# First layer's weight products moved into the adjacency build, and the last 96 nodes updated in three sets of 32

## The chip, the cores and the metric

The kernel runs on one core of a Trainium2 chip. The metric is the device time of one execution in microseconds (us). Before the change the median of 6 runs is 1797.62 us (1793.65 to 1804.84). In the profile the engines are PE (TensorE matmul), PEld (TensorE weight load), DVE (VectorE), ACT (ScalarE), POOL (GpSimd) and SP (SyncE).

## The reference, cut to what matters

A graph of 625 nodes with 512 features and 20000 edges, sorted by destination, goes through four layers, each on the normalised features of the one before, with a residual. All arrays are float32.

```python
edge_index = jnp.stack([src, dst])
h = jnp.maximum(_layernorm(x, axis=-1), 0.0)
x = x + _L0_gnn_ref(h, edge_index, L0_gnn_W, L0_gnn_b)
h = jnp.maximum(_layernorm(x, axis=-1), 0.0)
x = x + _L1_gnn_ref(h, src, dst, edge_type_8, edge_weight, ...)   # relational, two sublayers
h = jnp.maximum(_layernorm(x, axis=-1), 0.0)
x = x + _L2_gnn_ref(h, edge_attr_4, edge_attr_8, edge_index, ...)
h = jnp.maximum(_layernorm(x, axis=-1), 0.0)
x = x + _L3_gnn_ref(h, edge_index, edge_attr_64, ...)
```

Layer 0 (SAGE with the mean):

```python
    neighbor_mean = neighbor_sum / neighbor_count[:, None]
    h = jnp.concatenate([x, neighbor_mean], axis=-1)
    return h @ W.T + b
```

Layer 3 (messages of edges, then an update of nodes):

```python
    h = mish(edge_feat @ W1 + b1)
    messages = mish(h @ W2 + b2)
    agg = jax.ops.segment_sum(messages, dst, num_segments=x.shape[0])
    u = mish(jnp.concatenate([x, agg], axis=-1) @ W3 + b3)
    out = u @ W4 + b4
    y = x + out
    ...                         # layer norm of y with gamma and beta
```

## The kernel before

Nodes lie in 5 chunks (NC) of 125 (P), edges in 160 tiles (NT) of 125, features in 4 chunks (KD) of 128. The order of instructions on an engine is chosen by a scheduler at compile time, which goes by the written order and takes a later instruction where an earlier one isn't ready in its model. Instructions wrapped in `keep(...)` hold their written order on their engine. The matmuls are not wrapped; nearly everything of VectorE and ScalarE in the parts below is.

**The build of the adjacency** (`layers01_near`, lines 436 to 581). Sixteen stages of ten edge tiles make eight weighted adjacency matrices (`adj`) and one plain count of edges (`cnt`), source by destination. For each tile VectorE makes a one-hot of the sources (`ohs`, line 556, six buffers) and for five tiles at a time a right side `rh` (line 547, three buffers); PE adds 15 products of them (line 538) into five PSUM banks, one for each chunk of sources. PSUM has eight banks in this part, all in one pool with the tag `q`. When a stage is done, ScalarE copies the new columns of its banks into `adj` and `cnt` (`copied`, line 507) and VectorE adds the columns that overlap with the stage before (`added`, line 519). In written order that happens in the next stage: after its second one-hot the copies and the additions for chunks 0 and 1, after its fourth the additions for chunks 2 to 4. PE does the first three tiles of a stage for chunks 0 to 2 first, then for chunks 3 and 4. In stages 0, 1, 4, 7 and 10 the copying is preceded by a zero fill of a block of columns on ScalarE (`zeroed`, line 497). Stage 0 also makes the edges' coefficients (`coefficients`, line 457). At its end x is loaded (line 234) and the small weights of layer 2 (`layer2_weights`, 16 loads on SP). At the ends of stages 8 and 9 x is normalised: statistics on VectorE (line 242), square root and relu on ScalarE (lines 244 and 252).

**Layer 0** (lines 583 to 619). After the build the weights W are loaded, h is transposed (line 264, copied by line 265), the neighbours are counted by 25 products of `cnt` with a column of ones (line 595), the neighbours' sums are made transposed, 40 products of h with `cnt` (line 606, in 512 and 113 columns), and 40 products with the two halves of W (line 613) follow; VectorE scales by the reciprocal count and adds to x.

**Layer 1** (lines 621 to 673) normalises x, transposes it, loads its weights (`loop` and four of `basis`, 1 MB each) when the pools of layer 0 are released, and begins with the products of line 637.

**Layer 3** (`layer3_near`) runs over 40 groups of four edge tiles, software-pipelined over steps s: `first(s)` makes z (lines 1327 and 1332), `second(s-2)` its product with W2 (line 1346), `sent(s-4)` sums messages by destination for a window of 32 nodes (line 1370, four matmuls side by side in columns of the array), `collected(s-5)` transposes them into `mT` (lines 1380 and 1381). mish is made as z times a quotient: a bounded copy (`bounded`, line 1291) goes through Exp, Ln(1+.) and Tanh on ScalarE (`quotients`, lines 1299 to 1303), and VectorE multiplies (lines 1468 and 1477). The last group is done in two halves (lines 1490 to 1493, multiplied by line 1361). The node update of a chunk follows when its last window is in: `update_u` (line 1391, the mish of it by `quotients` and `update_mul`), `update_turn` (transpose), `update_out` (line 1422, with the layer norm's statistics) and `update_root`/`update_end` (norm and output). Chunks 0 to 3 are updated between steps; the last chunk of 125 nodes when all groups are done.

Of the kernel before, what the change touches and what calls it, by code (L numbers as in the profile page):

```python
# [194 lines left out]
def gnn_body(ctx: ExitStack, tc: tile.TileContext, a: dict, out: bass.AP, consts, near: bool):  # L195
# [34 lines left out]
    hT = node.tile([128, KD, N], F32, tag="hT", name="hT")  # L230
# [16 lines left out]
    def norm_relu(h, c, stats, keep=lambda i: i):  # L247
        mv, rstd = stats
        off = work.tile([P, 1], F32, tag="off1", name="off1", bufs=NC)
        keep(nc.vector.reciprocal(rstd, rstd))  # L250
        keep(nc.vector.scalar_tensor_tensor(off, mv[:, 0:1], -1.0, rstd, op0=ALU.mult, op1=ALU.mult))
        nc.scalar.activation(h[:, c, :], x[:, c, :], AF.Relu, bias=off, scale=rstd)
# [177 lines left out]
    def layers01_near(wts2):  # L430
# [5 lines left out]
        with tc.tile_pool(name="adjacency", bufs=1) as bp:  # L436
            adj = bp.tile([P, NC, NQ, N], F32, name="adj")
            with tc.tile_pool(name="counts", bufs=1) as cp:
                cnt = cp.tile([P, NC, N], F32, name="cnt")
                with tc.tile_pool(name="build", bufs=2) as lp, \  # L440
# [16 lines left out]
                    def coefficients(k0):  # L457
                        ks = slice(k0, min(k0 + 4, K))
                        n = ks.stop - k0
                        oh_r = lp.tile([128, 4, P], F32, tag="oh_r", name="oh_r")  # L460
# [16 lines left out]
                    eq = lp.tile([P, NT, WT], BF16, name="eq", bufs=1)  # L477

# [28 lines left out]
                    def copied(s):  # L507


                        if s in zeros:  # L510
                            zeroed(s)
# [7 lines left out]
                    def added(s, cs):  # L519
# [4 lines left out]
                        for c in cs:  # L524
                            for dst, v in ((adj[:, c, :, at][:, :, lo:hi], done[s][c][:P, :NQ, lo:hi]),
                                           (cnt[:, c, at][:, lo:hi], done[s][c][:P, NQ, lo:hi])):
                                keep(nc.vector.tensor_add(dst, v, dst))

                    for s in range(NS):
# [14 lines left out]
                        for j0, j1 in zip(parts_of, parts_of[1:]):  # L544
# [6 lines left out]
                            if s == 0 and j1 < GS:  # L551
                                hots(j1, 2 * j1 if j1 < 8 else NT)
                                coefficients(j1)
                            for j in range(j0, j1):
# [13 lines left out]
                                if s > 0 and j == 3:  # L568
                                    added(s - 1, (2, 3, 4))
                        if s == NS - 1:  # L570
                            copied(s)
                            added(s, range(NC))
                        if s == 0:
                            load_rest()
                            w2s = layer2_weights(wts2)
                        if s == NS // 2:
                            h = node.tile([P, NC, D], F32, tag="h", name="h")
                            stats = [norm_stats(c, keep) for c in range(NC)]
                        if s == NS // 2 + 1:
                            for c in range(NC):  # L580
                                norm_relu(h, c, stats[c], keep)

                with tc.tile_pool(name="layer0n", bufs=2) as lp, banks("z", 8):
                    w0 = [lp.tile([128, KD, D], F32, name=f"w0{i}", bufs=1) for i in range(2)]
                    for i in range(2):
                        nc.sync.dma_start(w0[i], chunks(a["L0_gnn_W"][i * D:(i + 1) * D, :]))
                    b0 = lp.tile([P, D], F32, name="b0", bufs=1)
                    nc.sync.dma_start(b0, bcast(a["L0_gnn_b"], D))
                    for c in range(NC):
                        transposed(hT, h[:, c, :], c)  # L590
                        nc.vector.tensor_add(x[:, c, :], x[:, c, :], b0)
                    pc = ps("pc")
                    for c in range(NC):
                        for s in range(NC):
                            nc.tensor.matmul(pc[:P, c:c + 1], cnt[:, s, c * P:(c + 1) * P], ones,
                                             start=s == 0, stop=s == NC - 1)
                    rc = lp.tile([P, NC], F32, tag="rc", name="rc")
                    nc.vector.tensor_scalar_max(rc, pc[:P, :NC], 1.0)
                    nc.vector.reciprocal(rc, rc)

                    sT = lp.tile([128, KD, N], F32, name="sT", bufs=1)
                    for f in range(KD):
                        for n0, n1 in ((0, 512), (512, N)):
                            p = ps("nsum")
                            for s in range(NC):
                                nc.tensor.matmul(p[:, :n1 - n0], h[:, s, f * 128:(f + 1) * 128],
                                                 cnt[:, s, n0:n1], start=s == 0, stop=s == NC - 1)
                            nc.scalar.copy(sT[:, f, n0:n1], p[:, :n1 - n0])
                    for c in range(NC):
                        for i, v in enumerate((hT, sT)):  # L610
                            p = ps("l0")
                            for k in range(KD):
                                nc.tensor.matmul(p[:P, :], v[:, k, c * P:(c + 1) * P], w0[i][:, k, :],  # L613
                                                 start=k == 0, stop=k == KD - 1)
                            if i == 0:
                                nc.vector.tensor_add(x[:, c, :], p[:P, :], x[:, c, :])
                            else:
                                nc.vector.scalar_tensor_tensor(x[:, c, :], p[:P, :], rc[:, c:c + 1], x[:, c, :],
                                                               op0=ALU.mult, op1=ALU.add)

            with tc.tile_pool(name="layer1n", bufs=1) as lp, banks("y", 3):
# [989 lines left out]
```

## Time and profile before

| | |
|---|---|
| median of 6 runs | 1797.62 us |
| the profiled execution's own time | 1803.98 us |
| its span (first to last instruction) | 1802.1 us |
| mean granted TensorE clock | 0.972 |
| PE / DVE / ACT / POOL busy | 1703.7 / 1012.3 / 761.6 / 809.8 us |
| last product of the build, first product of layer 1 on PE | 170.53, 251.29 us |
| last record of line 1346 (second products of layer 3) ends | 1763.6 us |

In the answers below a row of a timeline has the start and the length in us, the engine, the line of the kernel, the operation, what it writes and reads, the shape and how many instructions were merged; in brackets the idle time of the engine before it and what ended it. A row of the chain of waits has start, length, engine, tile and line. A row of a table by stretches has the stretch, its length, and for PE, PEld, DVE, ACT and POOL the busy time and the number of instructions, then the granted clock (1.00 is full), the DMA engines' busy share and GB/s. In a row of groups the last part is the idle time before its instructions. A float32 matmul of the program is two records in the profile.

### The profile page before, as it was taken

How to read it: one execution, taken by the hardware profiler on the slowest of the kernel's cores; microseconds unless marked ns; L12 is line 12 of the kernel's file. 1: busy time of each engine (PE TensorE's matmuls, PEld its weight loads, DVE VectorE, ACT ScalarE, POOL GpSimd, SP SyncE). 2: the span in 40 equal slices, each digit the busy share in tenths (PEclk: the TensorE clock that was granted, in tenths of full speed). 3: DMA queues.
4: the chain of work that ended last, by engine and by line, in shares of the span. 5: the costliest groups of instructions: out<-in, count | busy, mean ns of one | idle time of the engine just before them, and what ended most of it. 6: DMA issues, size and time to landing. Idle time of an engine off the chain costs nothing.

```text
span 1802.1 us, 24375 instructions
## 1 busy us (share of the span) xinstructions
PE 1703.7 (95%) x9770; PEld 882.1 (49%) x9770; DVE 1012.3 (56%) x1697; ACT 761.6 (42%) x792; POOL 809.8 (45%) x479
## 2 busy tenths in 40 slices
PE   4888999999999889999999899999999999999995
PEld 4878544444444334444554445445444544444443
DVE  7997110001000378877953666876676676667663
ACT  2352010000000312222213677776676777767664
POOL 0000000000000277665715788888887788778300
PEclk9999899999999789999999899999999999999997
DMA  2001030020000186757535588666675676667300
GB/s 74 3 3 54 1 122 24 0 93 6 0 0 0 53 203 169 174 148 168 144 90 143 102 159 154 124 129 111 114 137 111 115 133 120 109 112 140 51 1 14
DMA packets 157220, 162.59 MB, mean 90 GB/s; under 512 B 97547, under 2 KB 104060, under 8 KB 157097
## 3 DMA queue, kind: packets, MB, share of 16 engines
q0 software_dynamic: 131584, 119.48, 33.9%
q1 hardware_dynamic: 20100, 32.69, 5.9%
q10 hardware_dynamic: 5412, 8.77, 1.7%
q8 instruction: 79, 1.29, 0.3%
q14 instruction: 45, 0.36, 0.1%
HBM read 155.11 MB, written 5.12 MB: 89 GB/s over the span
## 4 chain that ended last, share of the span: by engine, by line
PE 85%; DVE 5%; DMA 3%; issue 3%; ACT 2%; POOL 1%; DVEq 0%; ACTq 0%; POOLq 0%; SPq 0%
PE z L1346 27%; PE agg L661 10%; PE hb L648 8%; PE sum L961 6%; PE tpw L938 4%; PE q L538 4%; PE z L1332 4%; PE z L1327 4%; PE mlp L890 2%; PE xsd L1040 2%; PE agg L637 2%; PE agg L1370 2%; PE l L613 2%; DMA g_s<-xd,dst_i 2%; POOL g_s L281 1%
## 5 line engine op out<-in xcount | busy, mean ns | idle before, releaser
L1346 PE MATMUL z<-wm,z 128*125 128x512 f32 x1280 | 558.2, 594 | 2.7 <-DVE z L1465 2.7
L1346 PEld LDWEIGHTS z<-wm,z 128*125 128x125 f32 x1280 | 238.1, 189 | 294.1 <-issue 270.8
L281 POOL DMA_INDIRECT g_s<-xs,src_i x160 | 300.2, 1876 | 124.1 <-issue 75.6
L281 POOL DMA_INDIRECT g_s<-xd,dst_i x144 | 304.4, 2114 | 46.0 <-issue 42.0
L902 POOL MEMSET mT<- 128x5000 f32 x1 | 4.3, 4265 | 589.9 <-PE tr L843 589.9
L281 POOL DMA_INDIRECT gup<-up,src_i x160 | 196.6, 1229 | 109.7 <-issue 39.7
L1348 DVE TENSOR_TENSOR mess<-z,b 125x512 f32<-125x512 f32 x160 | 106.3, 686 | 137.3 <-PE z L1346 137.3
L661 PE MATMUL agg<-hb,adj 125*125 125x512 f32 x400 | 173.6, 592 | 0.0
L651 DVE COPY hb<-hb 125x512 f32<-125x512 f32 x20 | 13.8, 691 | 263.0 <-PE hb L648 263.0
L945 DVE TENSOR_TENSOR msg<-tpw,gup 125x768 f32<-125x768 f32 x160 | 151.3, 945 | 0.0
L1334 DVE TENSOR_SCALAR z<-z,b 128x500 f32<-128x500 f32 (+1 forms) x164 | 108.4, 719 | 73.4 <-PE z L1332 71.6
L538 PE MATMUL q<-rh,ohs 125*128 125x96 bf16 (+1 forms) x2400 | 120.4, 213 | 27.6 <-DVE ohs L556 26.4
L1299 ACT ACTIVATE uz<-uz 128x2000 f32<-128x2000 f32 (+1 forms) x41 | 75.0, 1830 | 154.2 <-DVE uz L1291 154.2
L648 PE MATMUL hb<-basis,hT 128*125 128x512 f32 x320 | 138.6, 592 | 0.0
L538 PEld LDWEIGHTS <-ohs 125*128 125x128 bf16 x2400 | 115.4, 101 | 32.7 <-DVE ohs L556 32.4
L961 PE MATMUL sum<-msg,ohy 125*32 125x256 f32 (+2 forms) x1600 | 124.5, 389 | 0.0
L653 ACT COPY hb<-hb 125x512 f32<-125x512 f32 x20 | 11.7, 585 | 260.2 <-PE hb L648 240.2
L661 PEld LDWEIGHTS agg<-hb,adj 125*125 125x125 f32 x400 | 74.8, 188 | 94.7 <-issue 94.7
L961 PEld LDWEIGHTS sum<-msg,ohy 125*32 125x32 f32 x1600 | 74.2, 109 | 84.3 <-issue 58.7
L1299 ACT ACTIVATE um<-um 125x2048 f32<-125x2048 f32 x39 | 74.5, 1910 | 71.1 <-DVE um L1291 71.1
L938 PE MATMUL tpw<-w,hid 64*125 64x512 f32 x320 | 97.3, 649 | 5.6 <-DVE msg L945 5.6
L943 DVE TENSOR_TENSOR msg<-tpw,gup 125x256 f32<-125x256 f32 x160 | 66.4, 415 | 63.6 <-PE tpw L938 55.5
(210 smaller groups left out, 2221.2 us busy)
## 6 DMA issues: line engine op xcount, KB each, us to landing
rt<-in_edge_attr SPq DMA_DIRECT2D x76, 125.0 KB
basis<-in_L_gnn_basis SPq DMA_DIRECT2D x8, 1024.0 KB
gup<-up,src_i POOLq DMA_INDIRECT x160, 5.6
g_s<-xs,src_i POOLq DMA_INDIRECT x160, 7.9
g_s<-xd,dst_i POOLq DMA_INDIRECT x144, 8.9
w<-in_L_gnn_W SPq DMA_DIRECT2D x2, 1024.0 KB
loop<-in_L_gnn_loop SPq DMA_DIRECT2D x2, 1024.0 KB
w1ab<-in_L_gnn_W ACTq DMA_DIRECT2D x1, 2048.0 KB
```

The costliest lines, as they stand in the source:

```text
L281: return nc.gpsimd.indirect_dma_start(out=dst, out_offset=None, in_=table, in_offset=bass.IndirectOffsetOnAxis(ap=idx[:, t:t + 1], axis=0) ...
L538: nc.tensor.matmul(q[c][:, :n, o:o + WT], hot[j][:, c, :], rhs[j][:, q0:q0 + n, :], start=j + k == 0, stop=j == GS - 1 and k == 2, skip_gr ...
L648: nc.tensor.matmul(p[:P, :], hT[:, k, s * P:(s + 1) * P], basis[b][:, k, :], start=k == 0, stop=k == KD - 1)
L661: nc.tensor.matmul(acc[c], adj[:, s - 1, l * NB + b, c * P:(c + 1) * P], hb[:, b, :], start=False, stop=s == NC and b == NB - 1)
L938: nc.tensor.matmul(p[:P, :], hid[s // 2][s % 2][rws, i * P:(i + 1) * P], w4[rws].rearrange("p k u -> p (k u)"), start=True, stop=True)
L945: nc.vector.tensor_mul(m[:, :, 1:, :], pv[:, 2:4, None, :].to_broadcast([P, 2, 3, MUL]), g[:, None, 1:, :].to_broadcast([P, 2, 3, MUL]))
L961: nc.tensor.matmul(A[r * W:(r + 1) * W, cs, :], oh[:, j, q, :], v, start=j % G == 0 and r not in done, stop=j % G == G - 1, skip_group_che ...
L1299: keep(nc.scalar.activation(u, u, AF.Exp))
L1327: nc.tensor.matmul(pf[f][:, :ne], w[half, f * 128:(f + 1) * 128], rt[half, cols], start=True, stop=False)
L1334: keep(nc.vector.tensor_scalar(zv[:, n, f, :], pf[f][:, :ne], b1[:, f:f + 1], None, op0=ALU.add))
L1346: nc.tensor.matmul(p[:P, :], z[:, j // w, f, j % w * P:(j % w + 1) * P], wm2[:, f, :], start=f == 0, stop=f == KD - 1)
L1348: keep(nc.vector.tensor_add(m[:, j, :], p[:P, :], bc["b2"]))
```

## The change

*In layers 0 and 1.* x is loaded a second time, as h, at the start, and both halves of W as well; ScalarE makes h's statistics (sums through `accum_out`), and the relu of h runs in stage 0. In stage 1 h is transposed. The products h·Wb and h·Wa, ten units of four matmuls, are put behind tiles 4, 6, 8 and 9 of stages 2 to 10, the tenth unit behind the build; ScalarE copies each unit out of PSUM, h·Wb over h and h·Wa into `own`. After the build the plain counts are multiplied with h·Wb, and a column of ones beside it gives the number of neighbours. Layer 1's weights are asked for before that, and its products read another layout of the transposed features (`hTc`). The storage of `cnt` is reused for layer 1's `hb`; that of W's second half for the small weights of layer 2, which are loaded at the end of stage 8.

*In layer 3.* The last chunk is split: its first 29 nodes are updated as a chunk of their own between the steps, and the other 96 in three sets of 32, each set's product with W3 as soon as its window is in, with the four blocks of features side by side in the array. The rest of their update (mish, transpose, output) is made at once at the end. The last group's mish is done in three pieces instead of two; for the group before it a table set is loaded ahead and the bounded copy stands ahead of the multiplication of the group before that.

```diff
+                h1 = node.tile([P, NC, D + 1], F32, tag="h", name="h")
+                h = h1[:, :, :D]
...
+                nc.sync.dma_start(h, a["x"].rearrange("(c p) d -> p c d", p=P))
...
+                nc.sync.dma_start(w0b, chunks(a["L0_gnn_W"][D:, :]))
...
+                    nc.sync.dma_start(w0a, chunks(a["L0_gnn_W"][:D, :]))
...
                     def copied(s):
-                        if s in zeros:
+                        if s > 0 and s in zeros:
                             zeroed(s)
...
+                    zeroed(0)
...
+                    keep(nc.gpsimd.memset(h1[:, :, D:], 1.0))
+                    for c in range(NC):
+                        keep(nc.scalar.activation(h[:, c, :], h[:, c, :], AF.Copy, accum_out=sums[:, c:c + 1]))
+                    keep(nc.scalar.mul(sums, sums, -1.0 / D))
...
+                        keep(nc.scalar.activation(junk[:P], h[:, c, :], AF.Square, bias=sums[:, c:c + 1],
+                                                  accum_out=var[:, c:c + 1]))
+                    keep(nc.scalar.activation(var, var, AF.Sqrt, bias=eps, scale=1.0 / D))
+                    def normed():
+                        keep(nc.vector.reciprocal(var, var))
+                        keep(nc.vector.tensor_mul(sums, sums, var))
+                        for c in range(NC):
+                            keep(nc.scalar.activation(h[:, c, :], h[:, c, :], AF.Relu, bias=sums[:, c:c + 1],
+                                                      scale=var[:, c:c + 1]))
+                    def turned(c):
+                        p = pp.tile([128, 512], F32, tag="q", name="tr")
+                        for k in range(KD):
+                            nc.tensor.transpose(p[:, k * P:(k + 1) * P], h[:, c, k * 128:(k + 1) * 128],
+                                                ident[:P, :P])
+                        keep(nc.scalar.copy(hTc[:, c, :, :P],
+                                            p[:, :KD * P].rearrange("p (k n) -> p k n", k=KD)))
+                    products = [(i, c) for i in range(2) for c in range(NC)]
+                    def product(k, at_end=False):
+                        i, c = products[0]
+                        if k == 0:
+                            unit["p"] = pp.tile([128, 512], F32, tag="q", name="hw")
+                        p = unit["p"]
+                        nc.tensor.matmul(p[:P, :], hTc[:, c, k, :P], (w0a if i else w0b)[:, k, :],
+                                         start=k == 0, stop=k == KD - 1)
+                        if k == KD - 1:
+                            keep(nc.scalar.copy((own if i else h)[:, c, :], p[:P, :]))
+                            products.pop(0)
...
+                                if s == 1 and j > 4:
+                                    turned(j - 5)
+                                if 2 <= s < 11 and j in (4, 6, 8, 9):
+                                    product((4, 6, 8, 9).index(j))
...
+                            for k in range(KD):
+                                product(k)
...
-                            w2s = layer2_weights(wts2)
-                        if s == NS // 2:
-                            h = node.tile([P, NC, D], F32, tag="h", name="h")
-                            stats = [norm_stats(c, keep) for c in range(NC)]
+                        if s == 8:
+                            w2s = layer2_weights(w2_all)
...
+                    b0 = bias_of(a["L0_gnn_b"], "b0")
+                    weights = layer_weights(0)
...
+                            for s in range(NC):
+                                for i in (1, 0):
+                                    nc.tensor.matmul(p[i][:P, :H + i], cnt[:, s, c * P:(c + 1) * P],
+                                                     h1[:, s, i * H:(i + 1) * H + i], start=s == 0,
+                                                     stop=s == NC - 1)
...
+            ends = ((0, 1), (2,), (3,))
+            ND = 96
+            first_d = N - ND
+            def rows_of(c):
+                return P if c < NC - 1 else P - ND
...
+            def late_rows(i):
+                c, r0 = NC - 1, P - ND
+                if i == 0:
...
+                    keep(nc.sync.dma_start(late_nodes["y"], h[r0:, c, :]))
+                    keep(nc.sync.dma_start(late_nodes["x"], x[r0:, c, :]))
+                else:
+                    j = i - 1
+                    for r in range(KD):
+                        keep(nc.sync.dma_start(late_nodes["u"][r * W:(r + 1) * W, j * 128:(j + 1) * 128],
+                                               uh[r0 + j * W:r0 + (j + 1) * W, c, r * 128:(r + 1) * 128]))
+            def late_u(j):
+                p = ps("u")
+                at = first_d + j * W
+                for k in range(KD):
+                    for r in range(KD):
+                        nc.tensor.matmul(p[r * W:(r + 1) * W, :128], mT[:, k, at:at + W],
+                                         late["w"][:, k, r * 128:(r + 1) * 128], start=k == 0, stop=k == KD - 1,
+                                         skip_group_check=True, tile_position=(0, r * W))
+                u = late_nodes["u"][:, j * 128:(j + 1) * 128]
+                keep(nc.vector.tensor_add(u, p[:, :128], u))
...
+                if s - 3 == NG - 2:
+                    set_of_exp()
+                    us["m", s - 3] = bounded(flat(ms[s - 3]), P, G * D, "uz", 2)
                 if s - 4 in ms and s - 4 < NG - 1:
                     m = flat(ms[s - 4])
                     keep(nc.vector.tensor_mul(m, m, us.pop(("m", s - 4))))
...
-                for c in range(NC - 1):
+                for c in range(NC):
                     if s - 5 == last_of[c]:
                         update_u(c)
-            c = NC - 1
-            update_u(c)
-            quotients([us["u", c]])
...
+                for j in range(ND // W):
+                    if s - 5 == last_of_d[j]:
+                        late_u(j)
+            u = late_nodes["u"]
+            us["u"] = bounded(u, 128, KD * ND, "uu", 1)
+            quotients([us["u"]])
+            for c in (NC - 2, NC - 1):
+                update_root(c)
+            keep(nc.vector.tensor_mul(u, u, us.pop("u")))
+            uT = late_turn()
+            for c in (NC - 2, NC - 1):
+                update_end(c)
+            normed(NC, uT, late_nodes["y"], ND, 2)
+            update_root(NC)
+            update_end(NC)
```

## Prediction

> **What bounds the kernel now.** I read the page's busy line first (PE 95% of the 1802.1 us span), then the table by stretches with edges at the stages of the adjacency build, then the timelines of ScalarE, PE and VectorE there, then the groups of layer 0, then the chain of waits from 1640 us on. Three stretches carry the change: the build (11 to 172 us), layer 0's products behind it (172 to 251) and the end (1731 to 1802).
>
> ```profile
> core 0: us, PE busy (x) PEld busy (x) DVE busy (x) ACT busy (x) POOL busy (x), PEclk, DMA share, GB/s
> 92.50:100.80 8.30, 7.12 (x154) 6.82 (x152) 7.99 (x24) 7.84 (x13) 0.00 (x0) 1.00 0.01 2
> 100.80:113.00 12.20, 7.70 (x140) 7.40 (x138) 12.03 (x36) 3.79 (x16) 0.00 (x0) 0.84 0.01 2
> 113.00:122.60 9.60, 9.47 (x177) 9.28 (x175) 8.57 (x32) 5.40 (x15) 0.00 (x0) 0.85 0.01 2
> 172.50:186.00 13.50, 13.42 (x71) 13.45 (x72) 0.00 (x0) 2.69 (x5) 0.00 (x0) 0.55 0.48 168
> 186.00:210.00 24.00, 24.00 (x79) 12.75 (x80) 3.33 (x7) 3.10 (x7) 0.00 (x0) 0.89 0.00 0
> 210.00:245.00 35.00, 34.63 (x83) 14.93 (x81) 11.59 (x26) 4.68 (x9) 0.00 (x0) 1.00 0.00 1
> ```
>
> A stage of the build lasts 8.25 us. VectorE is busy 8.0 of it and sets the pace, but PE is busy 7.1: there is one microsecond of PE to give away per stage, not more. Stages 8 and 9 are longer because VectorE also does the node statistics. After the build PE alone works, and in the counting of neighbours at half clock.
>
> The groups of layer 0 (busy us, mean ns):
>
> ```profile
> L595 PE MATMUL pc<-ones,cnt 125*125 125x1 f32 x50 | 10.5, 345 | 0.0
> L606 PE MATMUL nsum<-cnt,h 125*128 125x512 f32 x40 | 20.5, 665 | 0.0
> L606 PE MATMUL nsum<-cnt,h 125*128 125x113 f32 x40 | 5.1, 274 | 0.0
> L613 PE MATMUL l<-w,hT 128*125 128x512 f32 x40 | 18.0, 592 | 0.0
> L613 PE MATMUL l<-w,sT 128*125 128x512 f32 x40 | 18.0, 592 | 0.0
> ```
>
> Two records make one fp32 product. The 80 of line 613 start every 0.43 us (34.4 us), so a product with a weight chunk costs 0.86 us.
>
> How a stage ends, and what ScalarE does in a stage that also zeroes a block of the adjacency:
>
> ```profile
> 161.76 0.38 ACT L517 COPY adj<-q 125x256 f32 x1 [6.68 <-DVE ohs L556]
> 163.37 2.47 PEld L538 LDWEIGHTS <-ohs 125*128 125x128 bf16 x54 [0.29 <-DVE ohs L556]
> 166.97 3.56 PE L538 MATMUL q<-rh,ohs 125*128 125x108 bf16 x75 [0.98 <-DVE ohs L556]
> ...
> 92.54 4.41 ACT L502 ACTIVATE adj<-iota_f 125x5000 f32<-125x5000 f32 x1 [0.79 <-DVE adj L527]
> 96.85 0.71 ACT L502 ACTIVATE cnt<-iota_f 125x625 f32<-125x625 f32 x1
> 97.96 0.38 ACT L517 COPY adj<-q 125x256 f32 x1 [0.41 <-PE q L538]
> ```
>
> Five tiles take PE 3.56 us (47.5 ns a product). The stage before ended on PE at 162.28 (its five tiles began at 158.72); ScalarE had begun to copy its banks at 161.76, VectorE adds two of them and only then makes the third one-hot, and PE goes on at 163.37, 1.6 us after ScalarE's first copy. The zero fill (92.54 to 97.56, 5.0 us) is done before the stage ends, in ScalarE's idle time: it costs nothing because ScalarE has nothing ahead of it that waits.
>
> **Part 1, what goes.** From PE's last build product (170.53) to the first product of layer 1 (251.29) are 80.8 us. In its place: the tenth unit of weight products, 4 x 0.86 = 3.4; its copy out of PSUM, 0.2 + 0.58 (row of line 653), which frees the banks; 50 products of the counts with h·W, 256 or 257 columns, 100 records. No row has that shape. Line 606 brackets it: 113 columns go at 0.18 us (24.4 us of the stretch less 40 x 0.43, over 40), which is the weight load's own 0.19; 512 go at 0.43. Stream and load overlap in both, so I take half of 0.43, 21.5 us (18 if loads bound it, 40 if they stopped overlapping). The separate count of neighbours (10.3 us) is one more column. Then reciprocal and two additions for the last chunk, 1.4; and normalising, transposing and copying it, 4.3 as from 245.42 to 249.69. The layer-1 weights, which PE waited for until 251.29, are asked for some 20 us ahead and are hidden by the count products (one MB landed 5.7 us after issue). Sum 31.4: **-49.4 us**. Statistics and normalisation leave VectorE's stages 8 and 9, 21.8 us instead of 16.5: **-5.3**.
>
> **Part 1, what comes.** Loading x as h, with both halves of W, moves to the head of SP's queue, in front of the edge attributes; layer 2's small weights, 16 issues, go back to stage 8, 400 us before they are used. ScalarE's statistics (ten passes of some 0.75, a table load of 1.28) end near 28 us, and VectorE needs them at 34 (it is then past line 472's last row, 33.6): hidden with 6 us to spare. If h came later than 24.8 each microsecond would count.
>
> Nine units of four products lie in stages 2 to 10, behind tiles 4, 6, 8 and 9. The first fills the 0.98 us in which PE waits for the sixth one-hot: free. The second and third come where PE has tiles waiting: 1.7 us. The fourth is behind the stage's last tile, and with it comes the wait that I think decides. ScalarE's order is held as written: the copy of the unit now stands ahead of the stage's bank copies. They begin 0.86 + 0.2 + 0.58 after the stage's last tile instead of 0.5 before it, 2.2 us later; behind them are VectorE's additions and the third one-hot, and PE, which has two or three free banks of eight, stops for it. A stage gets 3.9 us longer: 9 x 3.9 = **+35.1**.
>
> In stages 4, 7 and 10 the zero fill too is written behind that copy and ahead of the bank copies, so its cover is gone: 3 x 5.0 = **+15.1**. In stage 1 five groups of transposes (20 took 3.09, so 0.62 a group) lie behind tiles 5 to 9; four lengthen the stage by 2.5, the fifth holds up its copy, the fill and the bank copies: 0.62 + 0.2 + 0.58 + 5.0 + 0.5 = 6.9, together **+9.4**.
>
> These four stops leave PE idle 6 to 7 us. The row for that:
>
> ```profile
> 110.24 13.63 PE L538 MATMUL q<-rh,ohs 125*128 125x108 bf16 x225 [3.52 <-DVE ohs L556]
> ```
>
> After 3.52 us of idleness 225 products took 13.63 instead of 10.7, and the granted clock was 0.84 and 0.85. So 0 to 2.9 us each; I take 2, as some of it falls in a wait for VectorE: **+8**. The Trainium skill ("TensorE: Matmul & The Clock Gate", "HAM oscillation") says that an idle gap above some 3.4 us halves the clock until a window of that length has been busy; the trace agrees with the gap. By the page alone each stop would cost an estimated 1.7 us, 6.8 in all, and the forecast would be 1 us lower.
>
> Part 1: 35.1 + 15.1 + 9.4 + 8 - 49.4 - 5.3 = **+12.9**.
>
> **Part 2, the end.** The chain of waits:
>
> ```profile
> 1754.16 1.91 ACT um L1299
> 1771.79 2.19 PE agg L1370 x32
> 1775.21 5.21 PE u L1391 x8
> 1787.56 5.86 PE o L1422 x16
> ```
>
> The 29 first nodes of the last chunk become a chunk of their own: u (3.70 for eight records), transposes (0.5), o (3.45), whatever the number of nodes. The u lies ahead of the last group's second product, which ends at 1767.2 instead of 1763.6. Group 38's bound now comes before group 37's multiplication (2.28) on VectorE, and a table set is loaded ahead that serves Exp and Ln (lines 1490 and 1491 have no load between them), one load of 1.28 fewer: ScalarE is through group 38 at 1762.5, as before. The skill's "ScalarE: Activation LUTs" ("What ACT_TABLE_LOAD costs") gives 2.66 us for a switch, with a drain; here the next activation starts 1.3 us after the load's start, so the row decides; by the page 1.4 more would be saved. The last piece is bounded at 1768.6, and its Exp, Ln, load and Tanh end at 1773.2 instead of 1771.3. But VectorE's order is held: before the last multiplications stand the first set's addition (its product ends at 1770.7), group 38's multiplication, and the 29 nodes' addition and statistics behind their o (until 1774.2), which ends near 1776.5. Then 2.5 for three multiplications and 0.5 for the sums: 1779.4 against 1773.98, +5.4. From there to the end of o were 19.4 us. Now two sets of 32, each an addition, 16 products and an addition (1.08 to 2.19 for the products, the two rows of line 1370 at full and low clock), bound, three activations on 384 columns with one load (2.8), multiplication, three transposes, copy and the same o (5.86): 15.5 to 17.7. Net +1.5 to +3.7; I take **+2.6** (-3 to +5, if PE takes the pieces in another order). The 14 small copies between buffers go to SP in stages 14 to 17 of layer 3, where it has loads queued two stages ahead: nothing, or 1 us if one blocks. Ending two chunks (3.2) hides under o.
>
> **Sum.** +15.5 on the profiled 1803.98 gives 1819.5. That execution lies 6.4 above the median, 1797.62, of the runs shown: 1813.1.
>
> **Rivals.** *The fourth product runs early.* PE's matmuls aren't held to the written order as ScalarE's and VectorE's are:
>
> ```profile
> 716.03 1.05 PE L890 MATMUL mlp<-ef,w 8*64 8x500 f32 x2
> 723.33 1.06 PE L890 MATMUL mlp<-ef,w 8*64 8x500 f32 x6
> ```
>
> A group of eight was split there, with other lines between. If all four products stand before tile 5, the unit's copy and most of the fill are past when the stage ends: 2.6 a stage (23.4), 2.9 for each of three fills, 4.5 in stage 1, no cold clock: 36.6 - 54.7 + 2.6 = -15.5, 1782. It decides from the point where the last matmul of a unit is ahead of tile 7. Against it: PE has tiles ready from tile 5 on, so nothing invites the move. *Half of it*, with only the last two matmuls one or two tiles earlier: 3.1 a stage, 3 a fill, 6 in stage 1, 3 of cold clock: 45.9 - 54.7 + 2.6 = -6, 1791. *The products aren't hidden at all* but nothing stops either: 36 x 0.86 + 2.5 = 33.5, 1779: even then faster. So the sign hangs on ScalarE's order alone. *h late*: 3.3 MB at 345 GB/s (the rate at the loads before layer 1) land by 23; against it the 24.8 above; each us late adds one.
>
> **How the numbers follow.** Forecast 0.57, with its own range from no cold clock and an early end (1800) to 2.9 each and a late end (1822). Early fourth product or nothing stopped 0.29 (1775 to 1787), half of it 0.12 (1788 to 1799), h late 0.02 (to 1826). What 0.3%, 5.4 us, can tell: faster below 1792.2: 0.29 + 0.05; within: 0.07 of the half and 0.02 of the forecast's edge; slower: 0.57. The range leaves out the lowest of the rival and the last case: 1778 to 1823.
>
> **What would show it.** Stages 2 to 10 near 12 us, 4, 7 and 10 near 17 to 19, with ScalarE's fill between the unit's copy and the bank copies and PE waiting for the third one-hot; the granted clock under 0.9 behind those; 31 us from PE's last build tile to layer 1; the last group's sums 5 us later and the end 2 to 4 shorter. Wrong, if the fill lies ahead of the unit's copy in time, or the stages take 11 us or less.

## The result and the profile after

The changed kernel takes 1812.09 us (median of 20 runs, 1807.02 to 1817.74) against 1797.92 of before (46 runs): a ratio of 1.0079, with a 95% interval of 1.0069 to 1.0089, that is 12.4 to 16.0 us slower. The profiled execution lies lower than its median, at 1806.83 us with a span of 1805.0; the two profiled spans differ by only 2.9 us. The layers between the two changed parts, whose work is unchanged, took 9 us less in this execution than in that of before, so the changed stretches are read by themselves and not through the spans.

The table by stretches of the kernel after, over three stages of the build (one that waits for a zero fill, the one behind it, an ordinary one) and from the last product of the build to layer 1:

```profile
core 0: us, PE busy (x) PEld busy (x) DVE busy (x) ACT busy (x) POOL busy (x), PEclk, DMA share, GB/s
84.38:100.75 16.37, 10.93 (x158) 8.33 (x159) 7.99 (x23) 7.30 (x15) 0.00 (x0) 0.98 0.01 1
100.75:113.46 12.71, 12.15 (x159) 9.54 (x160) 8.00 (x23) 2.41 (x14) 0.00 (x0) 0.89 0.01 3
156.45:167.94 11.49, 10.93 (x159) 8.33 (x160) 8.01 (x23) 2.42 (x14) 0.00 (x0) 1.00 0.01 3
226.60:254.40 27.80, 25.54 (x122) 20.92 (x122) 18.60 (x58) 7.36 (x20) 0.00 (x0) 1.00 0.58 208
```

VectorE has the 8.0 us of work in a stage that it had before, but no longer sets the pace: an ordinary stage is 11.49 us long and PE is busy for 10.93 of it. A stage with a zero fill is 4.88 us longer with the same work on PE, and the one behind it runs at a granted clock of 0.89. The end of such a stage, PE and ScalarE from their timelines (the second PE row is an ordinary boundary):

```profile
94.37 0.59 ACT L586 COPY h<-hw 125x512 f32<-125x512 f32 x1 [9.07 <-PE q L598]
94.85 4.40 ACT L516 ACTIVATE adj<-iota_f 125x5000 f32<-125x5000 f32 x1
99.14 0.71 ACT L516 ACTIVATE cnt<-iota_f 125x625 f32<-125x625 f32 x1
99.75 0.37 ACT L531 COPY adj<-q 125x256 f32 x1
...
100.75 4.08 PE L598 MATMUL q<-rh,ohs 125*128 125x108 bf16 x57 [5.31 <-DVE cnt L541]
156.45 2.17 PE L598 MATMUL q<-rh,ohs 125*128 125x108 bf16 x42 [0.43 <-DVE cnt L541]
```

The unit's copy, then the whole fill, then the first bank copy: PE stands 5.31 us for a bank that those copies and VectorE's additions free. Without a fill between, it stands 0.43. The prediction had PE waiting for the third one-hot; the row names VectorE's additions (line 541), which come ahead of that one-hot.

In the tail the trace has a wait that the prediction does not have. VectorE, ScalarE and PE, from their timelines:

```profile
1746.82 0.41 DVE L1364 TENSOR_SCALAR uu<-u 29x512 f32<-29x512 f32 x1 [16.68 <-PE o L1506]
...
1750.79 1.91 ACT L1381 ACTIVATE um<-um 125x2048 f32<-125x2048 f32 x1 [22.71 <-DVE um L1364]
...
1749.49 1.08 PE L1455 MATMUL agg<-mess,oh 125*32 125x128 f32 x32 [2.60 <-DVE mess L1601]
1753.50 16.77 PE L1428 MATMUL z<-wm,z 128*125 128x512 f32 x32 [2.93 <-DVE mess L1430]
```

The bounded copy of the 29-node chunk writes a tile of the tag `uu`, of which there is one buffer. The transposed updates of chunk 3 lie in it until their product with the output weights has run, and PE has that product behind 32 of line 1428. VectorE waits 16.68 us; a multiplication of messages, the copy that ScalarE waits 22.71 us for, a multiplication of z and the additions that free PE's banks (line 1430) stand behind it in the held order, and PE stops twice. The 32 products behind the stops take 16.77 us. Before, the same products had no stop ahead of them and took 13.90:

```profile
1749.73 13.90 PE L1346 MATMUL z<-wm,z 128*125 128x512 f32 x32
```

The chain of waits at the end:

```profile
1786.86 1.28 ACT L1385
1788.15 0.53 ACT uu L1385
1788.71 0.57 DVE w_all L1654
...
1789.32 0.91 PE tr L1548 x3
1790.26 0.57 DVE uT L1550
1790.87 6.55 PE o L1506 x16
```

From the end of the last group's sums (1781.48) to the end of the span are 23.5 us; before, from 1773.91, they were 28.2.

### The profile page after: what moved, and what is told of

The parts are those of the page before. It is cut to its first block, busy times and chain, and to the rows that moved or that the text cites. A ratio compares the mean times of both kernels' runs of the same rounds, so it can differ in the third digit from the quotient of the medians.

```text
span 1805.0 us, 24600 instructions
## 1 busy us (share of the span) xinstructions
PE 1699.2 (94%) x9847; PEld 882.5 (49%) x9847; DVE 1014.2 (56%) x1706; ACT 770.7 (43%) x818; POOL 809.4 (45%) x480
## 4 chain that ended last, share of the span: by engine, by line
PE 87%; DVE 4%; ACT 3%; DMA 2%; issue 2%; POOL 1%; DVEq 0%; ACTq 0%; POOLq 0%; SPq 0%
PE z L1428 30%; PE agg L730 10%; PE hb L717 8%; PE sum L1034 6%; PE q L598 6%; PE z L1409 4%; PE tpw L1011 4%; PE z L1414 4%; PE agg L1455 2%; PE xsd L1113 2%; PE hw L583 2%; PE agg L706 2%; PE mlp L963 2%; PE o L1506 1%; DMA gup<-up,src_i 1%
## 5 line engine op out<-in xcount | busy, mean ns | idle before, releaser
L282 POOL DMA_INDIRECT g_s<-xs,src_i x160 | 295.8, 1849 | 123.0 <-issue 76.0
L730 PE MATMUL agg<-cnt,adj 125*125 125x512 f32 x400 | 173.6, 592 | 0.0
L598 PE MATMUL q<-rh,ohs 125*128 125x96 bf16 (+1 forms) x2400 | 132.6, 217 | 40.2 <-DVE cnt L541 25.3
L598 PEld LDWEIGHTS <-ohs 125*128 125x128 bf16 x2400 | 125.4, 103 | 67.3 <-issue 36.5
L720 DVE COPY cnt<-hb 125x512 f32<-125x512 f32 x20 | 13.8, 692 | 256.3 <-PE hb L717 256.3
L1381 ACT ACTIVATE uz<-uz 128x2000 f32<-128x2000 f32 (+2 forms) x42 | 76.9, 1831 | 149.4 <-DVE uz L1364 149.4
L730 PEld LDWEIGHTS agg<-cnt,adj 125*125 125x125 f32 x400 | 74.7, 188 | 94.8 <-issue 94.8
L722 ACT COPY cnt<-hb 125x512 f32<-125x512 f32 x20 | 11.7, 585 | 253.5 <-PE hb L717 253.5
L1011 PE MATMUL tpw<-w_all,hid 64*125 64x512 f32 x320 | 98.8, 648 | 4.5 <-DVE msg L1018 4.5
```

The costliest lines, as they stand in the source:

```text
L282: return nc.gpsimd.indirect_dma_start(out=dst, out_offset=None, in_=table, in_offset=bass.IndirectOffsetOnAxis(ap=idx[:, t:t + 1], axis=0) ...
L598: nc.tensor.matmul(q[c][:, :n, o:o + WT], hot[j][:, c, :], rhs[j][:, q0:q0 + n, :], start=j + k == 0, stop=j == GS - 1 and k == 2, skip_gr ...
L730: nc.tensor.matmul(acc[c], adj[:, s - 1, l * NB + b, c * P:(c + 1) * P], hb[:, b, :], start=False, stop=s == NC and b == NB - 1)
L1011: nc.tensor.matmul(p[:P, :], hid[s // 2][s % 2][rws, i * P:(i + 1) * P], w4[rws].rearrange("p k u -> p (k u)"), start=True, stop=True)
L1381: keep(nc.scalar.activation(u, u, AF.Exp))
```

## The experiments

Twelve kernels ran in three sets of four; each set ran on one chip together with the kernel before, and its ratio is to those runs. Two stretches of each profile are compared with before's: the time at which layer 1's first product starts (251.29 us before), and the tail, from the transposes of chunk 3 to the end (1729.60 to 1802.1: 72.5 us before). The last column is the timed difference, the ratio less 1 times the median of before in that set.

| run | start of layer 1 | tail | both | ratio (95% interval) | timed |
|---|---|---|---|---|---|
| e1_tail_only | -0.3 | +8.3 | +8.0 | 1.0021 (1.0004 to 1.0038) | +3.8 |
| e2_first_only | +3.3 | +1.3 | +4.6 | 1.0031 (1.0012 to 1.0051) | +5.6 |
| e3_fill_early | -21.4 | +8.2 | -13.2 | 0.9932 (0.9909 to 0.9954) | -12.4 |
| e4_uT_own | +4.2 | +0.4 | +4.6 | 1.0029 (1.0007 to 1.0051) | +5.3 |
| a0_after | +4.0 | +9.2 | +13.2 | 1.0092 (1.0072 to 1.0111) | +16.5 |
| e1b_tail_only | +0.1 | +8.7 | +8.8 | 1.0047 (1.0030 to 1.0065) | +8.4 |
| b1_all_mended | -21.0 | +2.5 | -18.5 | 0.9914 (0.9894 to 0.9933) | -15.4 |
| b2_mended_old_end | -21.2 | +0.7 | -20.5 | 0.9894 (0.9873 to 0.9915) | -19.0 |
| c1_fourth_early | -28.9 | +8.4 | -20.5 | 0.9903 (0.9885 to 0.9920) | -17.5 |
| c2_best_old_end | -19.0 | -0.1 | -19.1 | 0.9900 (0.9883 to 0.9917) | -18.0 |
| c3_best_new_end | -18.1 | +2.3 | -15.8 | 0.9915 (0.9897 to 0.9933) | -15.3 |
| c4_best_warm | -20.9 | -0.4 | -21.3 | 0.9883 (0.9866 to 0.9899) | -21.1 |

The two stretches account for the timed difference within about 4 us in every row. Before's medians were 1819.09, 1796.11 and 1799.9 us in the three sets.

**The two parts apart.** Each kernel has the last layer of the one version and the first layers of the other; the buffer of the late loads is named to fit.

```diff
-    layer3_near of before                  (e1_tail_only, e1b_tail_only: the rest of before)
+    layer3_near of after
-    layer3_near of after                   (e2_first_only: the rest of after)
+    layer3_near of before
```

> Before, with only the last part of the change (the three sets of 32 nodes and the new order around group 38 and 39). The theory now held: the bounded copy of the 29-node chunk takes the one buffer that the transposed updates of chunk 3 still hold, VectorE stands 16.7 us behind it, TensorE loses 2.60 + 2.93 us for that, and the rest is the longer way of the last group: 7 to 9 us over before, 1805 to 1807. The forecast on record had +2.6 for this part: 1800.5. A third reading, that the 8.95 us between the two profiled executions' tails is chance: no difference.

> After, with before's last layer: only the first part of the change. The theory now held: the build grows by 56.1 us in the profiled execution and 53 come back behind it, and with the two parts' sum at 14.2 by the medians this part is worth +5 to +7: 1803 to 1805. The forecast on record had +12.9: 1811. If the parts work on each other (the clock that the last layer is granted, for one), the sum of this run's and the tail's differences is not 14.2.

> The last part of the change alone, again: the profile had 80.8 us for the tail against 72.5 of before, but the times gave only +0.7 to +6.9. If the 8.3 us of the trace are the price, the ratio is 1.0035 to 1.0055 (6.5 to 10 us); if something ahead of the tail gives a part back, it is 1.001 to 1.003.

> The changed kernel as it is, beside the others on one chip. If the ratio to before depends on the chip, it lies away from 1.0079 here; if not, within 1.0055 to 1.0100. Its tail (from the transposes of chunk 3 to the end) should take 81 us again, and TensorE stand 5.2 to 5.3 us at each of the four zero fills, both of which are settled by the order of instructions.

The last part alone cost 3.8 us at first, below the 7 to 9 expected, and 8.4 us in the second set; the tail was 80.8 and 81.2 us long in the two profiles, which is what after has. The times of the first set (0.7 to 6.9 us) would fit the forecast's +2.6 as well; the two tails and the times of the second set (5.4 to 11.7) do not. The first part alone cost 5.6 us (2.2 to 9.3). With the second measurement the parts make 14.0, with the first 9.4, and the whole change is 14.2: within these intervals nothing shows that the parts work on each other. The changed kernel came out at 1.0092 in the second set, in accord with 1.0079.

**The zero fill out of the way.**

```diff
                     def copied(s):
-                        if s > 0 and s in zeros:
-                            zeroed(s)
...
                                 if s > 0 and j == 3:
                                     added(s - 1, (2, 3, 4))
+                                    if s in zeros:
+                                        zeroed(s)
```

> After, with ScalarE's zero fill of stages 1, 4, 7 and 10 issued after the fourth one-hot of the stage before's additions, so that it no longer stands between the unit's copy and the bank copies. Theory: the 5.2 to 5.3 us that TensorE stands idle at each of the fills go down to the 0.4 us of an ordinary boundary (4 x 4.9 = 19.6), and with them most of the slow matmuls behind (57 matmuls in 4.1 to 5.0 us): 15 to 24 us less than after, 1788 to 1797. Rival: ScalarE is full, the fill holds up the unit's copy instead and the bank copies with it: within 3 us of after. Second rival: only the gap goes and the clock does not come back: 12 to 15 us.

The table by stretches of that run, over the same kind of stages (the first makes the fill, the second is ordinary):

```profile
78.49:89.98 11.49, 10.93 (x158) 8.34 (x159) 7.99 (x23) 7.43 (x15) 0.00 (x0) 1.00 0.00 1
89.98:101.47 11.49, 10.93 (x158) 8.33 (x159) 8.00 (x23) 2.42 (x13) 0.00 (x0) 1.00 0.02 4
```

PE at the end of the stage with the fill, and layer 1's first product, here and (last row) in after:

```profile
89.98 2.17 PE L596 MATMUL q<-rh,ohs 125*128 125x108 bf16 x42 [0.43 <-DVE cnt L539]
...
229.89 2.74 PE L706 MATMUL agg<-loop,hT 128*125 128x512 f32 x6
...
254.36 2.74 PE L706 MATMUL agg<-loop,hT 128*125 128x512 f32 x6
```

ScalarE does the same fill (7.43 us of work against 2.42), the stage has not grown, and PE stands 0.43 us at its end instead of 5.31. Layer 1 starts 24.5 us earlier than in after, just above the 15 to 24 expected: 4 stops of 4.88 us, 19.5, and 5.0 of the slow matmuls behind them (1.2 in each stage behind a fill, 12.71 against 11.49). This one move turns a kernel that is 0.8% slower into one that is 0.7% faster. The fill costs nothing as long as it does not stand in front of the bank copies; both rivals fall.

**A buffer for the transposed updates.**

```diff
-                uT = lp.tile([128, D], F32, tag="uu", name="uT", bufs=1)[:, :KD * n]
+                uT = lp.tile([128, D], F32, tag="uT", name="uT", bufs=1)[:, :KD * n]
```

> After, with a buffer of its own for the transposed updates, so that the 29-node chunk's bounded copy need not wait for chunk 3's product. Theory: the 16.68 us wait on VectorE goes, and TensorE's stalls of 2.60 and 2.93 us with it: 4 to 7 us less than after, 1805 to 1808. Rival: VectorE is only held later in the same group, by the exponentials that ScalarE has in its kept order, and the end is set by the 32-row sets behind the last group: within 2 us of after.

VectorE and PE in that run's timelines:

```profile
1749.36 0.42 DVE L1364 TENSOR_SCALAR uu<-u 29x512 f32<-29x512 f32 x1
...
1765.90 1.08 PE L1455 MATMUL agg<-mess,oh 125*32 125x128 f32 x32
1766.91 0.33 PE L1465 MATMUL trs<-ident,ag 128*128 128x128 f32 x1
1767.07 13.90 PE L1428 MATMUL z<-wm,z 128*125 128x512 f32 x32
```

The bounded copy follows at once on the addition that feeds it, PE goes on without a stop, and line 1428 is back at 13.90 us. The tail is 72.9 us instead of 81.45: the wait cost 8.6 us, more than the 4 to 7 expected, of which 5.5 were PE's two stops and 2.9 the slower products behind. By the times, this run (+5.3) and the first part alone (+5.6) agree, so with the buffer the new tail costs nothing that these times can tell (each is known to about 4 us).

**The node features ahead of the weights, and the two mended versions.** b1 and b2 have the early fill, the weights' loads written behind stage 0, and layer 2's small weights written into stage 12; b1 has the new end with the buffer, b2 the old end.

> After with four edits: the zero fills early, the transposed updates in a buffer of their own, the node features loaded ahead of both halves of the first weights (which are asked for behind the build's first stage), and layer 2's small weights asked for in stage 12 instead of 8. By the terms measured so far, against before: -24.5 of the fills and +3 of the first part as it is, so -21.4; -4.1 if the late node features go; -1.2 for the small weights' wait; +0.4 for the tail: -26, a ratio of 0.9855. If the node features are not what held up stage 0, 0.988. If the clock or a wait in the later layers gives the gain back, above 0.992, as the first mended run's -12 with a tail of +8 leaves possible.

> The same, but with the last layer as it was before the change. If the three sets of 32 at the end are worth nothing once their wait is gone (72.86 us against 72.5), this and the run with the new end agree within 3 us. If they were worth the 4 to 5 us by which the stretch from the last sums to the end is shorter, this one is 4 to 5 slower.

Both come within about 3 us of what their stretches say, 7 to 11 us short of the 26 expected. Layer 1 starts no earlier than with the early fill alone (-21.0 and -21.2 against -21.4), so neither the features' edit (4.1 expected) nor that of the small weights (1.2) brought anything. The scheduler issued the weights' loads 4 us behind the features' all the same, and ScalarE began on h at 27.88 us, as in after (27.93). The new end was 3.3 us slower than the old one by the medians, 1.8 by the tails, with intervals that overlap: with its wait gone it still brings nothing.

The next edit holds the loads back by a dependence (a copied element of h, overwritten by the load), and holds the scaling of layer 2's weights in stage 12:

```diff
+                nc.gpsimd.tensor_copy(w0b[:P, 0, :1], h[:, 0, :1])
                 nc.sync.dma_start(w0b, chunks(a["L0_gnn_W"][D:, :]))
...
-        nc.vector.tensor_scalar_mul(w4[:, :3, :], w4[:, :3, :], s4)
+        tc.keep_in_program_order(nc.vector.tensor_scalar_mul(w4[:, :3, :], w4[:, :3, :], s4))
```

> First part of the change with the early fills, both halves of the first weights loaded only when the node features are there, and layer 2's small weights scaled on VectorE only in stage 12; the last layer as before the change. The earlier mended run still asked for both weights some 4 us behind the node features, which began to be used at 27.88 us, as without the edit. Theory: the features land some 6 us sooner, TensorE goes on after the build's stage 0 at 41 instead of 45.7, and stage 7's boundary loses its 0.8 us: 5 us less than the earlier mended run with the old end, a ratio to before of 0.9865. Rival: it is not the transfers that share the rate but the features' own 1.25 MB; then TensorE goes on at 45 again, 0.989.

> The same with the three sets of 32 at the end and the transposed updates in a buffer of their own. By the two earlier mended runs (0.9914 and 0.9894) the new end costs 0 to 4 us even without its wait: 0 to 4 us over the run with the old end. If the tail alone decides (72.9 us against 72.5), within 1.5.

GpSimd and VectorE in c2's timelines, and a row of its table by stretches:

```profile
24.48 0.18 POOL L451 COPY w_all<-h 125x1 f32<-125x1 f32 x1 [20.17 <-DMA h<-in_x]
24.61 0.81 POOL L465 MEMSET parts<- 125x160 bf16 x1
...
25.45 1.41 DVE L607 TENSOR_TENSOR rh<-eq,parts 125x1200 bf16<-125x1200 bf16 x1 [7.64 <-POOL h L547]
...
12.00:24.60 12.60, 2.04 (x8) 1.77 (x8) 3.81 (x8) 5.36 (x3) 0.12 (x1) 1.00 0.32 119
```

The copied element shows when h landed: 24.48, 3.45 us before its first use in after, not the 6 expected. With the weights held back the queues moved 119 GB/s from 12.0 to 24.6 us, the features' 1.25 MB and the 0.3 MB of the edge attributes, so the features' own load takes most of that time; the rival is mostly right. The gain was lost to a wait that the edit made: the memset of `parts`, done at 11.04 in after, now stands behind the copied element on GpSimd, VectorE waits 7.64 us for it, and PE passes stage 0 at 48.91 us instead of 45.20. The small weights' wait, 0.8 to 1.2 us at one boundary, is gone (0.43 there now). The new end was 2.7 us slower than the old one by the ratios (the intervals overlap), 2.4 by the tails. Most of that is in the products of the last two sets with W3, first e4, whose tail was 72.9 us, then c3:

```profile
1792.79 1.08 PE L1538 MATMUL u<-wm3b,aT 128*32 128x128 f32 x32 [0.61 <-DVE aT L1466]
1794.51 1.08 PE L1538 MATMUL u<-wm3b,aT 128*32 128x128 f32 x32 [0.38 <-DVE aT L1466]
...
1759.22 1.94 PE L1540 MATMUL u<-wm3b,aT 128*32 128x128 f32 x32 [0.61 <-DVE aT L1468]
1761.94 1.93 PE L1540 MATMUL u<-wm3b,aT 128*32 128x128 f32 x32 [0.39 <-DVE aT L1468]
```

The code of the tail is the same, and the granted clock over the same six us of it was 1.00 in e4 and 0.65 in c3; b1 is like c3. Why the clock differs there from one execution to the next is not shown.

**The fourth product earlier.** With the early fill.

```diff
-                                if 2 <= s < 11 and j in (4, 6, 8, 9):
-                                    product((4, 6, 8, 9).index(j))
+                                if 2 <= s < 11 and j in (4, 5, 6, 7):
+                                    product((4, 5, 6, 7).index(j))
```

> After with the early zero fills, and the four products of a unit behind tiles 4, 5, 6 and 7 instead of 4, 6, 8 and 9, so that the unit's copy is done before the stage's last tile. The forecast charged 2.2 us a stage to the copy standing ahead of the bank copies: by that a stage of 11.49 us falls to 9.3, and the run lies 15 to 20 us under the early fills alone. The theory now held is that TensorE's own work fills the stage (11.06 busy of 11.49, with 0.43 of waiting), so that no more than 0.43 a stage can go: 11.06 to 11.5 us a stage, 0 to 4 us in all.

Two stages by stretches:

```profile
66.39:77.20 10.81, 10.66 (x159) 8.22 (x160) 8.02 (x23) 2.20 (x10) 0.00 (x0) 1.00 0.01 2
88.04:99.05 11.01, 10.66 (x159) 8.22 (x159) 8.01 (x23) 2.59 (x12) 0.00 (x0) 1.00 0.02 4
```

The copy is out of the way and the stage still takes 10.8 to 11.0 us, with PE busy for 10.66: eight stages between 66.39 and 153.15 us take 10.85 each. So of the 3.24 us by which an ordinary stage of after exceeds the old 8.25, 0.64 goes with the copy's place and 2.6 stays, nearly all of it PE's own work. The build ends 7.4 us before that of the early fill alone (194.70 against 202.12); the ratios of the two sets differ by 5 us. That is more than the 0 to 4 expected, as PE's work in a stage came to 10.66 us and not 11.06, and far from the 15 to 20 of the forecast's reading.

**The idle time at the end filled.** c3 with

```diff
+            idle = ps("idle")
+            for k in range(5):
+                nc.tensor.matmul(idle, late["wm4"][:, 0, :128], late["wm4"][:, k % KD, :], start=True, stop=True)
             quotients([us["u"]])
```

> The same with five products of no use (128x512, 0.86 us each at full clock) given to TensorE in the 4.4 us in which it waits for the last sets' exponentials. If the last product's 6.5 us (granted clock 0.57) come from the idle time ahead of it, it takes 3.5 to 4.5 us and the kernel ends 2 to 3 us earlier than without them. If they come from something else (the three small transposes ahead, the copy's wait), it stays at 5 to 6.5 us and nothing changes.

PE at the end, first c3, then c4:

```profile
1768.25 0.90 PE L1550 MATMUL tr<-ident,w_all 128*128 128x128 f32 x3 [4.37 <-DVE w_all L1656]
1769.80 6.12 PE L1508 MATMUL o<-wm,uT 128*96 128x256 f32 x16 [0.65 <-DVE uT L1552]
```

```profile
1759.51 4.95 PE L1655 MATMUL idle<-wm 128*128 128x512 f32 x10
1764.30 0.49 PE L1550 MATMUL tr<-ident,w_all 128*128 128x128 f32 x3
1765.44 3.69 PE L1508 MATMUL o<-wm,uT 128*96 128x256 f32 x16 [0.65 <-DVE uT L1552]
```

Ten records of useless products stand where PE idled, and the last product takes 3.69 us instead of 6.12 (at a granted clock of 1.00 instead of 0.60), the transposes 0.49 instead of 0.90. In both kernels the two sets ahead of it took 1.93 to 1.94 us each, so this compares like with like. From the end of the last set's sums (1763.87 and 1759.58) to the end of the span are 19.8 us in c3 and 17.2 in c4: 2.6 us, as expected of the idle time. The medians differ by 6.9 (1785.35 against 1778.46); in the two profiles 2.7 us more lie ahead of layer 1, where the code is the same in both, and some 1.6 are not placed. This kernel has the lowest ratio to before, 0.9883 (0.9866 to 0.9899), though most of the other mended runs' intervals overlap with its own. The early fourth product was not tried together with it.

## Why the prediction was right, and where it was not

The sign and the place were right, and so was the mechanism that decides the sign: in ScalarE's order the fill stood ahead of the bank copies, and moving that one call turned the sign. The largest term of the sum, the +35.1 of the ordinary stages, had most of its mechanism wrong, as said below. That the total was hit is luck: part 1 was forecast 9.8 us too high (12.9 against 3.1) and part 2 some 6 too low (2.6 against 8.95).

**Part 1, what goes.** Forecast 31.4 us from the last product of the build to layer 1, measured 27.7 (226.63 to 254.36), a gain of 53.1 instead of 49.4. The bracketed price of the count products held: 21.5 against 21.86. Among what was charged too much is the tenth unit, half of which PE ran inside stage 15.

**Part 1, what comes.** Forecast +62.3 us on the build (the 67.6 of the four terms less the 5.3 of the statistics), measured +56.1. Ordinary stage: +3.9 forecast, +3.24 measured. This is the mis-sized term, 5.9 us over nine stages. The forecast let PE stop at once for the late bank copies (2.2 us); in fact PE runs 18 products of the next stage meanwhile (1.27 us), in the banks that are free, and waits 0.43. c1 puts the copy's place at 0.64 a stage; the rest is PE's. The fills: 5.0 forecast, 4.88 measured. Stage 1: +9.4 forecast, 14.6 us instead of 8.25 measured, +6.3. The cold clock: +8 forecast, 5.0 shown by the early fill. Put at nothing in the forecast: at one boundary VectorE has to scale layer 2's small weights, whose load is late, and PE stands 1.65 us there instead of 0.43.

**h late.** What the forecast gave 0.02 came true: against its threshold of 24.8 us, h was used at 27.93, VectorE stood 2.62 us at the reciprocal, and stage 0 ended 4.1 us later (45.20 against 41.08). The rate of 345 GB/s was read from several weight loads of 1 MB in flight; in c2 the features' load, with only the edge attributes' beside it, ran at 119, with the 16 DMA engines busy for 0.32 of the time (0.89 and 295 GB/s for the weights from 26 to 29 us). So the rate was not shared away: this load by itself keeps only a third of the engines busy. Why, no run here shows.

Together part 1 is +3.1 in the profiled execution (+4.0 in the repeat, +5.6 timed) against the forecast's +12.9.

**Part 2.** Forecast +2.6, measured +8.95. The step that failed is the one that made the 29 nodes a chunk of their own: it priced u, transposes and o of the chunk and not the buffer that they pass through. Without that wait (e4) the steps held: the sums of the last group 5.1 us later (5.4 forecast), the stretch behind them 4.8 shorter (1.7 to 3.9 forecast), together +0.4. "ScalarE is through group 38 at 1762.5, as before" fell with the wait: it began on group 37 only at 1750.79 and was through group 38 at 1769.08, which is 12.6 us later than before, counted from the start of the tail; in e4 it was 0.5 later.

**The rivals.** That the fourth product runs early, or half of it, did not happen: in PE's order it stands behind all 150 products of its stage. What it would bring with the fills left where they are was not run. "The products aren't hidden at all" describes the ordinary stages better than the forecast's own words: most of their 3.24 us is PE's work. The measured sign came from the fills and the clock behind them (24.5 us, e3); without the tail's wait alone the kernel stays slower (e4, +5.3).

## What to carry to other kernels

In an engine whose order is held, ask of each instruction put in what stands behind it that another engine waits for: a copy of 0.6 us with a fill of 5 us behind it costs 5 us when both come ahead of the copies that free the banks, and nothing when the fill is written eight tiles earlier. When a loop body is run once more at another time, follow every tile tag with one buffer to its last reader; the price of the instructions says nothing of that wait. Before charging a wait to an engine, count what it can still do with the buffers that are free.

## What the runs showed of the hardware that was not expected

Two stops of 2.60 and 2.93 us with 1.07 us of products between were enough to bring the clock down. The tail of after by stretches, ahead of the stops, at them and behind:

```profile
1732.00:1746.00 14.00, 14.00 (x34) 6.20 (x33) 0.00 (x0) 0.00 (x0) 0.00 (x0) 1.00 0.00 0
...
1749.50:1753.50 4.00, 1.07 (x32) 0.80 (x33) 4.00 (x4) 2.69 (x3) 0.00 (x0) 0.85 0.02 6
1753.50:1762.00 8.50, 8.50 (x14) 3.65 (x15) 6.51 (x11) 8.44 (x7) 0.00 (x0) 0.67 0.00 0
```

The granted clock was 0.67 in the stretch behind, and the 32 products there took 2.9 us longer; without the stops (e4) they took 13.90 us, as before. The Trainium skill ("TensorE: Matmul & The Clock Gate", "HAM oscillation") warns of idle gaps above some 3.4 us; each of the two here was shorter, and the clock fell all the same. Whether one of them alone would do it, no run here shows.

Useless products were a cheap remedy at the end of this kernel: five of them in a wait of 4.4 us gave 2.6 us back (c4 against c3).

From the last product of layer 1 to the first of layer 3 it took 371 to 379 us in the four profiles of the first set and 358.7 to 362.7 in the others, before's among them, with the same work. No profile of before was taken in the first set; that its median was 1819.09 there fits a stretch as much longer, and it is why only ratios within a set are compared.
